# A graph layer on one core: TensorE's small products stand in four groups between its big tiles, not seven, and some work of the last pairs moves ahead

## The chip, the core and the metric

The kernel runs on one core of a Trainium2 chip. Its time is device microseconds of one execution: a median of 3041.12 us over three runs (3034.78 to 3041.24). The core's engines run side by side and wait for each other through semaphores: TensorE (PE) multiplies matrices into PSUM, VectorE (DVE) and ScalarE (ACT) work elementwise, GpSimd (POOL) issues the gathers from memory, SyncE (SP) issues most other transfers. Each engine takes its instructions in the order in which they were written, so an instruction that waits holds all behind it.

## What is computed

There are 12,500 nodes with 32 features and 400,000 edges (src, dst) sorted by dst, each with 32 features of its own.

```python
h = max(layernorm(x), 0)
e = concat(h[src], h[dst], edge_attr)            # 400000 x 96
v = relu(e @ W1 + b1) @ W2 + b2                  # 64 hidden, 32 out
out = x + max(segment_max(v, dst), h)
```

The work per edge is: fetch two rows of h, multiply 96 by 64, multiply 64 by 32, and take the maximum over the edges of one dst.

## The kernel before, in words

**Chunks.** The edges are cut into four stripes, one on each 32 partitions, and each stripe into 196 chunks of 512 edges. One pass of the main loop (`for c in range(0, NCH, 2)`, 98 passes) takes a pair of chunks c and c + 1 through the products, and prepares a = c + 2 and b = c + 3. In the text a0 to a3 and b0 to b3 are the four tiles of chunk a and of chunk b.

**Rows of src, two ways.** A chunk needs 16 x 128 rows h[src]. Twelve of the sixteen are gathered from memory by GpSimd (`gather`, L168), one indirect transfer for 128 rows, so 24 a pass. The other four are made by TensorE (`tile`, L279): the node table `hs` lies in SBUF in two parts, and a one-hot matrix `hot` picks groups of 14 nodes out of it in 14 products of 128 x 128 by 128 x 448; VectorE masks the result (L286), takes the maximum over the group (L287), and turns rows into features (`to_features`, L300 and L303). The one-hots are made by VectorE (`one_hots`, L248) and ScalarE (`one_hots_act`, L257 and L258).

**Small products.** Between these tiles TensorE does, once a pass, seven further groups:

- ea (`edges_into`, L644): W1's part for edge features of chunks a and b, into the banks `ph`; 16 records of 32 x 64 by 32 x 512.
- of (`windows_into`, L644): W1's part for h[dst], by way of one-hots `of` against the 32 rows of dst that a stripe's chunk spans.
- ht (L644): W1's part for h[src] of chunks c and c + 1; it closes the banks.
- pv (L710): W2, after ScalarE's relu (`hid`, L695).
- the transposes of `leave_1` (L551, 128 x 128): they turn the running maxima `sm` of the pair, which VectorE's scans (L717) made, from features to edges; VectorE adds b2 (L553, `so`).
- two groups of `leave_2` (L565), one for each chunk of a pair: a one-hot `last` (`lasts`, L539) picks the last edge of every dst. `leave_3` copies both results with ScalarE (L584, `wo`) and stores the spans to `top_d` with eight transfers of SP (L589). For the last eight chunks (from `LATE`) it keeps them in SBUF instead, and `late_out` scatters them into the output with GpSimd (L636).

**Order.** The order of all engines is the order of the source text: the kernel runs under a manual schedule. In the pass of before it is, on TensorE: ht, a1, pv, a2, ea, a3, L565, b0, L565, b1, of, b2, transposes, b3, a0 of the next pair. Transposes and L565 groups of a pair are thus one pass apart: the transposes of c and c + 1 stand in pass c, their L565 groups in pass c + 2. All tiles, transposes, pv results and L565 results share three PSUM buffers, `pv`.

**Waits put in by hand.** `HELD` says for some gathers of a pair after which product of an earlier pass they may start (`hold`, `passes`); the first gather waits for `of` of three passes ahead.

**End.** The nodes' rows come back from `top_d` in three shares (`rows_of`), and `finish` takes the maximum with h, adds x and stores them (L605 to L607). `finish(0)` and `finish(1)` are in pass LATE + 2, `finish(2)` in pass LATE + 4 (c = 192). After that `rows_next` gathers one span (`ew`, L623), and seven scatters of the late chunks follow (L636).

Of the kernel before, what the change touches and what calls it, by code (L numbers as in the profile page):

```python
# [24 lines left out]
P = 128  # L25
# [12 lines left out]
NCH = 196  # L38
# [16 lines left out]
LATE = NCH - 8  # L55
PIECE = 2 * A0
GP = 3
HELD = {0: (3, 'of'), 2: (3, 'b2'), 4: (3, 'b3'), 6: (3, 'n0'), 8: (2, 'ht'), 10: (2, 'a1'), 12: (2, 'pv'), 14: (2, 'a2'), 16: (2, 'a3'), 18: (2, 'lv'), 20: (2, 'b0'), 22: (2, 'b1')}
ROUND = 12582912.0
LOW = 1e30  # L60
BY_ACT = range(A1 - 3, A1)
# [10 lines left out]
def gnn_kernel(ctx, tc, x, src, src_mm, src_t, dst, dst_ext, lo, lo_c, ends_b, edge_attr, weights, w1, w2, b2, out):  # L72
# [19 lines left out]
    nc = tc.nc  # L92
# [108 lines left out]
    def passes(iteration, name, ins):  # L201

        passed[iteration, name] = ins
# [64 lines left out]
    def tile(c, m):  # L268

        if c not in MMC:  # L270
            return
        if m == 0:
            mm_rows[c] = early.tile([P, MM, D], F32, name="gm", bufs=6)
        hot = hots[c]
        e = slice(m * P, (m + 1) * P)
        po = early_ps.tile([P, C], F32, name="pv", bufs=3)[:, :D * A0]
        for k in range(A1):
            for part in range(2):
                ins = nc.tensor.matmul(po, hot[:, k, e], hs[:, part, k].rearrange("p f a -> p (f a)"),  # L279
                                 start=(k == 0 and part == 0), stop=(k == A1 - 1 and part == 1))  # L280
        if m == 0 and c % 2 == 0:
            passes(c // 2 - 2, "n0", ins)
        passes(c // 2 - 1, "ab"[c % 2] + str(m), ins)
        of_group = po.rearrange("p (f a) -> p f a", a=A0)
        one = early.tile([P, D, A0], F32, name="one", bufs=2)
        nc.vector.tensor_tensor(one, of_group, masks[c][:, m, None, :].to_broadcast([P, D, A0]), op=ALU.mult)  # L286
        nc.vector.tensor_reduce(mm_rows[c][:, m, :], one, axis=AX.X, op=ALU.max)  # L287
# [190 lines left out]
    with tc.tile_pool(name="edges", bufs=3) as pool, tc.tile_pool(name="edges_ps", bufs=1, space=PSUM) as ps:  # L478
# [57 lines left out]
        def lasts(c):  # L536
            last = pool.tile([P, J, NS, W], F32, name="last", bufs=2)
            at = ats[c // BLOCK].rearrange("p (s c) j -> p s c j", s=NS)[:, :, c % BLOCK].rearrange("p s j -> p j s")
            nc.vector.tensor_tensor(last, count_ps[:, None, None, :].to_broadcast([P, J, NS, W]),  # L539
                                    at[:, :, :, None].to_broadcast([P, J, NS, W]), op=ALU.is_equal)  # L540
            return last
# [4 lines left out]
        def leave_1(c, sm):  # L546

            px = early_ps.tile([P, C], F32, name="pv", bufs=3).rearrange("p (j q) -> p j q", j=J)
            n = blocks(c)
            for j in range(n):  # L550
                passes(c // 2, "tr", nc.tensor.transpose(px[:, j, :], sm[:, j * P:(j + 1) * P], ident))  # L551
            so = pool.tile([P, J, P], F32, name="so", bufs=2)
            nc.vector.tensor_tensor(so[:, :n], px[:, :n], b2r[:, None, :].to_broadcast([P, n, P]), op=ALU.add)  # L553
            return so

        def leave_2(c, x, sos, last):

            n = 1 + (c < NCH - 2)
            if x == 0:
                left[c] = early_ps.tile([P, C], F32, name="pv", bufs=3)[:, :n * 2 * D]  # L560
            pw = left[c]
            to = x % n * 2 * D
            for j in range(blocks(c + x)):
                for g in range(2):
                    ins = nc.tensor.matmul(pw[g * 2 * W:(g + 1) * 2 * W, to:to + 2 * D],  # L565
                                           last[x][:, j, 2 * g:2 * g + 2].rearrange("p s w -> p (s w)"),
                                           sos[x][:, j, g * 2 * D:(g + 1) * 2 * D], start=(j == 0 and x < n),
                                           stop=(j == blocks(c + x) - 1 and x >= 2 - n))
            passes(c // 2 + 1, ("lv", "lw")[x], ins)

        def leave_3(c):

            n = 1 + (c < NCH - 2)
            pw = left.pop(c)
            if c >= LATE:
                late[c] = ow = pool.tile([P, 2, D], F32, name="ow", bufs=4)
                pw = pw.rearrange("p (x k f) -> p x k f", k=2, f=D)
                for s in range(NS):
                    g = slice(s * W, (s + 1) * W)
                    nc.vector.tensor_tensor(ow[g, :n], pw[g, :, s % 2], late_x[c][g, 1, :n], op=ALU.max)  # L580
                nc.vector.tensor_tensor(ow[:, :n], ow[:, :n], late_x[c][:, 0, :n], op=ALU.add)
                return
            wo = pool.tile([P, 4 * D], F32, name="wo")
            nc.scalar.activation(wo, pw, AF.Copy)  # L584
            for x in range(2):
                base = windows.pop(c + x)
                for s in range(NS):
                    g = slice(s * W, (s + 1) * W)
                    nc.sync.dma_start(top_d[bass.ds(base[s], W), :],  # L589
                                      wo[g, (2 * x + s % 2) * D:(2 * x + s % 2 + 1) * D])  # L590
# [11 lines left out]
        def finish(i):  # L602

            r, (t, of_h) = shares.pop(i)
            nc.vector.tensor_tensor(t, t, of_h, op=ALU.max)  # L605
            nc.vector.tensor_tensor(t, t, xs[:, r], op=ALU.add)
            nc.sync.dma_start(out_v[:, r], t)  # L607
# [20 lines left out]
        def late_out(c):  # L628

            ow = late.pop(c)  # L630
            n = 1 + (c < NCH - 2)
            k = c - LATE
            if n == 1:
                nc.vector.tensor_tensor(ow[:, 0], ow[:, 0], ew, op=ALU.max)
            for x in range(n):
                nc.gpsimd.indirect_dma_start(  # L636
                    out=out[:, :], out_offset=bass.IndirectOffsetOnAxis(ap=late_o[:, k + x:k + x + 1], axis=0),
                    in_=ow[:, x, :], in_offset=None)
# [8 lines left out]
        def edges_into(c):  # L647

            if c < NCH:
                two = [ps.tile([P, 2, C], F32, name=f"ph{k}") for k in range(NS // 2)]  # L650
                ph = [two[s // 2][:, s % 2] for s in range(NS)]
                banks[c] = two
                passes(c // 2 - 1, "ea", into_ph(ph, [(w1c, loaded[c + x][0]) for x in range(2)], True, False))
                return ph

        def windows_into(c, ph):
            if c < NCH:
                passes(c // 2 - 1, "of", into_ph(ph, [(spans[c // 2][:, x], ofs.pop(c + x)) for x in range(2)],
                                                 False, False))
# [9 lines left out]
        ph = edges_into(0)  # L669
# [10 lines left out]
        for c in range(0, NCH, 2):  # L680
# [6 lines left out]
            if c % LOAD and b_next < NB and b_next not in ats and b_next not in loaded_b:  # L687
                load_block(b_next)

            ht = [hts.pop(c + x).rearrange("p k e -> p (k e)") for x in range(2)]  # L690
            passes(c // 2, "ht", into_ph(ph, [(w1a, ht[x]) for x in range(2)], False, True))
            hid = []
# [8 lines left out]
                flag = nc.values_load(general_i[0:1, 0:1], min_val=0, max_val=P)  # L701
            one_hots_act(b)
            one_hots(b, 0, 2)
            tile(a, 1)
            to_features(a, 1)
            pv = [early_ps.tile([P, C], F32, name="pv", bufs=3) for x in range(2)]
# [12 lines left out]
                sms.append(sm)  # L719
            tile(a, 2)  # L720
            to_features(a, 2)
            last = [lasts(c - 2 + x) for x in range(2)] if c else []
            ph = edges_into(a)
            one_hots(b, 2, BY_ACT.start)
            mask_of(b)
            tile(a, 3)
# [1 line left out]
            load_keys(a + KEYS)  # L728
            to_features(a, 3)
            to_features(a, J)  # L730
            if c:
                leave_2(c - 2, 0, so, last)
            if c == LATE + 4:
                finish(2)
            tile(b, 0)
            to_features(b, 0)
            if c:
                leave_2(c - 2, 1, so, last)
                leave_3(c - 2)
            one_hots(a + 2, 0, 2)  # L740
            if c == LATE + 2:
                finish(0)
            tile(b, 1)
            to_features(b, 1)
            windows_into(a, ph)
            one_hots(a + 2, 2, BY_ACT.start)
            mask_of(a + 2)
            tile(b, 2)
            to_features(b, 2)
            so = [leave_1(c + x, sms[x]) for x in range(2)]  # L750
            if c == LATE:
                half = LOAD * C // 2
                db = pool.tile([P, LOAD * C], I32, name="db", bufs=2).bitcast(F32)
# [36 lines left out]
        for ins, at in waiting:  # L790
            if at not in passed:
                continue
            tc.add_manual_dep(ins.ins, passed[at].ins.name,
                              mybir.DependencyInfo(mybir.DependencyClass.Sync, mybir.DependencyReason.DATA))
        last = [lasts(NCH - 2 + x) for x in range(2)]
        late_out(LATE + 4)
        for x in range(2):
            leave_2(NCH - 2, x, so, last)
        leave_3(NCH - 2)
# [145 lines left out]
```

## Time and profile before

| | |
|---|---|
| median of three runs | 3041.12 us |
| the profiled execution | 3041.33 us, span of its instructions 3039.6 us |
| TensorE busy (matmul) | 2941.8 us, 97% |
| GpSimd busy | 2239.7 us, 74% |
| VectorE busy | 2147.8 us, 71% |
| ScalarE busy | 1330.9 us, 44% |
| mean granted clock of TensorE | 0.986 |

Lines of the order of time give start, length, engine, line of the source, operation, the tile written and those read, and in brackets the idle time of the engine before it and what ended it. Successive instructions of one kind are merged (x14). A matrix product's length overlaps with the next one's start, so the distance between starts tells what a group costs. An fp32 product on TensorE leaves two records here, so the eight calls of a small group stand as x16. Lines of a stretch (A:B) give its length and each engine's busy time in it with the count of instructions, then TensorE's granted clock.

### The profile page before, as it was taken

How to read it: one execution, taken by the hardware profiler on the slowest of the kernel's cores; microseconds unless marked ns; L12 is line 12 of the kernel's file. 1: busy time of each engine (PE TensorE's matmuls, PEld its weight loads, DVE VectorE, ACT ScalarE, POOL GpSimd, SP SyncE). 2: the span in 40 equal slices, each digit the busy share in tenths (PEclk: the TensorE clock that was granted, in tenths of full speed). 3: DMA queues.
4: the chain of work that ended last, by engine and by line, in shares of the span. 5: the costliest groups of instructions: out<-in, count | busy, mean ns of one | idle time of the engine just before them, and what ended most of it. 6: DMA issues, size and time to landing. Idle time of an engine off the chain costs nothing. (4 is left out here: it accounts for less than half of the span.)

```text
span 3039.6 us, 59462 instructions
## 1 busy us (share of the span) xinstructions
PE 2941.8 (97%) x21067; PEld 2280.2 (75%) x21067; DVE 2147.8 (71%) x3885; ACT 1330.9 (44%) x1977; POOL 2239.7 (74%) x2380
## 2 busy tenths in 40 slices
PE   2899999999999999999999999999999999999997
PEld 1677777777777777777777777777777777777775
DVE  5577767677777676777777776777777767777666
ACT  3444444444444444444444444444444444444432
POOL 7677777777777777777777777777777777777762
PEclk7899999999999999999999999999999999999998
DMA  5422222222222223222222222222222222222222
GB/s 200 106 73 71 77 63 75 70 73 66 78 78 64 70 72 81 59 73 75 74 62 77 70 77 64 74 70 73 69 80 75 59 76 74 77 60 75 67 56 70
DMA packets 188988, 228.10 MB, mean 75 GB/s; under 512 B 119037, under 2 KB 160397, under 8 KB 175886
## 3 DMA queue, kind: packets, MB, share of 16 engines
q10 hardware_dynamic: 25076, 107.07, 11.0%
q0 software_dynamic: 75552, 38.83, 8.7%
q1 hardware_dynamic: 88058, 78.37, 8.3%
q8 instruction: 165, 2.70, 0.4%
q14 instruction: 137, 1.12, 0.1%
HBM read 211.79 MB, written 12.22 MB: 74 GB/s over the span
## 5 line engine op out<-in xcount | busy, mean ns | idle before, releaser
L168 POOL DMA_INDIRECT gh<-h_d,src_i x2321 | 2192.8, 945 | 734.0 <-issue 564.5
L279 PE MATMUL pv<-hs,hot 128*128 128x448 f32 x10808 | 2355.1, 370 | 0.9 <-DVE one L286 0.9
L279 PEld LDWEIGHTS pv<-hs,hot 128*128 128x128 f32 x10808 | 1979.0, 188 | 464.8 <-DVE one L286 234.9
L286 DVE TENSOR_TENSOR one<-pv,mask 128x448 f32<-128x448 f32 x772 | 482.2, 625 | 781.2 <-PE pv L279 772.6
L258 ACT ACTIVATE hot<-away,ones 128x512 fp32r<-128x512 f32 x579 | 418.8, 723 | 429.3 <-issue 409.5
L695 ACT ACTIVATE hid<-ph,wt 128x1024 f32<-128x1024 f32 x196 | 207.7, 1111 | 767.5 <-PE ph L644 761.6
L287 DVE TENSOR_REDUCE gm<-one 128x32 f32<-128x448 f32 x772 | 478.8, 620 | 26.5
L248 DVE TENSOR_TENSOR hot<-kb,consts 128x1024 fp32r<-128x1024 f16 (+1 forms) x385 | 458.2, 1190 | 0.0
L257 ACT ACTIVATE away<-kb,key_n 128x512 f32<-128x512 f16 x579 | 410.7, 709 | 0.0
L717 DVE TENSOR_TENSOR_SCAN sm<-pb,sm,pv 128x512 f32<-128x512 bf16 x195 | 245.0, 1257 | 18.9 <-PE pv L710 8.3
L300 DVE STREAM_TRANSPOSE ht<-gh 128x96 f32<-128x96 f32 x774 | 207.8, 268 | 0.0
L533 ACT ACTIVATE of<-db,below 128x512 f32<-128x512 int32 x196 | 139.5, 712 | 102.4 <-PE ph L644 97.7
L565 PEld LDWEIGHTS pv<-so,last 128*64 128x64 f32 x3128 | 107.5, 138 | 64.7 <-issue 64.7
L534 ACT ACTIVATE of<-of,ones 128x512 f32<-128x512 f32 x196 | 141.9, 724 | 6.4
L565 PE MATMUL pv<-so,last 128*64 128x64 f32 x3128 | 134.2, 229 | 4.5 <-DVE last L539 4.5
L644 PE MATMUL ph<-of,qw 32*64 32x512 f32 x1568 | 111.4, 617 | 24.1 <-ACT of L534 24.1
L644 PE MATMUL ph<-ea,wt 32*64 32x512 f32 x1568 | 110.1, 617 | 20.7 <-DMA qf<-q_d 20.7
L531 ACT ACTIVATE qw<-qf 128x128 f32<-128x128 f32 x98 | 30.4, 310 | 226.2 <-DMA top_d<-wo 127.3
L553 DVE TENSOR_TENSOR so<-pv,wt 128x512 f32<-128x512 f32 x196 | 122.3, 663 | 3.4 <-PE pv L551 3.3
L539 DVE TENSOR_TENSOR last<-consts,at 128x512 f32<-128x512 f32 x196 | 122.5, 663 | 0.0
L644 PE MATMUL ph<-ht,wt 32*64 32x512 f32 x1568 | 113.0, 622 | 3.2 <-DVE ht L306 3.2
L710 PE MATMUL pv<-hid,wt 64*32 64x512 f32 x1568 | 109.5, 606 | 2.7 <-ACT hid L695 2.7
(93 smaller groups left out, 599.6 us busy)
## 6 DMA issues: line engine op xcount, KB each, us to landing
ea<-in_edge_attr SPq DMA_DIRECT2D x49, 1024.0 KB
db<-in_dst_ext ACTq DMA_DIRECT2D x48, 1024.0 KB
gh<-h_d,src_i POOLq DMA_INDIRECT x2321
pb<-pen_d ACTq DMA_DIRECT2D x48, 512.0 KB
kb<-key_d ACTq DMA_DIRECT2D x47, 512.0 KB
qf<-q_d SPq DMA_DIRECT2D x784, 8.0 KB
top_d<-wo SPq DMA_DIRECT2D x752, 4.0 KB
q_d<-qs SPq DMA_DIRECT2D x6, 512.0 KB
```

The source lines that it names most:

```text
L168: ins = nc.gpsimd.indirect_dma_start(out=parts[-1][:, i, :], out_offset=None, in_=h_d[:, :], in_offset=bass.IndirectOffsetOnAxis(ap=src_i[ ...
L248: nc.vector.tensor_tensor(hot_of(c)[:, start:stop], keys[c][:, None, :].to_broadcast([P, n, MM * P]), key_ps[:, start:stop, None].to_broad ...
L257: nc.scalar.activation(away, keys[c], AF.Square, bias=key_n[:, k:k + 1])
L258: nc.scalar.activation(hot_of(c)[:, k], away, AF.Relu, bias=ones, scale=-1.0)
L279: ins = nc.tensor.matmul(po, hot[:, k, e], hs[:, part, k].rearrange("p f a -> p (f a)"), start=(k == 0 and part == 0), stop=(k == A1 - 1 a ...
L286: nc.vector.tensor_tensor(one, of_group, masks[c][:, m, None, :].to_broadcast([P, D, A0]), op=ALU.mult)
L287: nc.vector.tensor_reduce(mm_rows[c][:, m, :], one, axis=AX.X, op=ALU.max)
L300: nc.vector.transpose(ht[:, r].rearrange("p k e -> p (k e)"), gh[c][part][:, :r.stop - r.start].rearrange("p k f -> p (k f)"))
L565: ins = nc.tensor.matmul(pw[g * 2 * W:(g + 1) * 2 * W, to:to + 2 * D], last[x][:, j, 2 * g:2 * g + 2].rearrange("p s w -> p (s w)"), sos[x ...
L644: ins = nc.tensor.matmul(ph[s][x * HID:(x + 1) * HID], w[g], e[g], start=start, stop=stop)
L695: nc.scalar.activation(two, of, AF.Relu, bias=b1c)
L717: nc.vector.tensor_tensor_scan(sm[:, :n], loaded.pop(c + x)[2][:, :n], pv[x][:, :n], before, op0=ALU.add, op1=ALU.max)
```

## The change

On TensorE the pass is now: transposes of the pair before and ht; a1; pv; a2, a3; ea and the first L565 group; b0, b1; of and the second L565 group; b2, b3, a0 of the next pair. Line by line:

- `leave_1` moves from behind b2 to the beginning of the next pass, ahead of ht. The last pair has its own call behind the loop.
- `edges_into` moves from between a2 and a3 to behind a3, next to the first `leave_2`.
- the second `leave_2` and `leave_3` move from behind b0 to behind `windows_into`, ahead of b2.
- `lasts` is called for c and c + 1 there too, for use one pass later, instead of behind a2 of the pass that uses it.
- `finish(2)` moves from behind a3 to behind a2 of its pass; `finish(0)` from behind b0 to ahead of it.
- in the last pass the L565 groups, `leave_3` and `late_out` of chunks 192 and 193 stand ahead of pv, and `lasts` of the last two chunks behind them.
- in `HELD` the first gather of a pair waits for the second L565 group instead of `of`.

```diff
-HELD = {0: (3, 'of'), 2: (3, 'b2'), ...
+HELD = {0: (3, 'lw'), 2: (3, 'b2'), ...
...
+            so = [leave_1(c - 2 + x, sms[x]) for x in range(2)] if c else []
             ht = [hts.pop(c + x).rearrange("p k e -> p (k e)") for x in range(2)]
             passes(c // 2, "ht", into_ph(ph, [(w1a, ht[x]) for x in range(2)], False, True))
...
+            if c == NCH - 2:
+                for x in range(2):
+                    leave_2(c - 2, x, so, last)
+                leave_3(c - 2)
+                late_out(c - 2)
+                last = [lasts(c + x) for x in range(2)]
             tile(a, 1)
...
             tile(a, 2)
             to_features(a, 2)
-            last = [lasts(c - 2 + x) for x in range(2)] if c else []
-            ph = edges_into(a)
+            if c == LATE + 4:
+                finish(2)
             one_hots(b, 2, BY_ACT.start)
...
             to_features(a, 3)
             to_features(a, J)
-            if c:
+            ph = edges_into(a)
+            if c and c < NCH - 2:
                 leave_2(c - 2, 0, so, last)
-            if c == LATE + 4:
-                finish(2)
+            if c == LATE + 2:
+                finish(0)
             tile(b, 0)
             to_features(b, 0)
-            if c:
-                leave_2(c - 2, 1, so, last)
-                leave_3(c - 2)
             one_hots(a + 2, 0, 2)
-            if c == LATE + 2:
-                finish(0)
             tile(b, 1)
             to_features(b, 1)
             windows_into(a, ph)
+            if c and c < NCH - 2:
+                leave_2(c - 2, 1, so, last)
+                leave_3(c - 2)
+            if c < NCH - 2:
+                last = [lasts(c + x) for x in range(2)]
             one_hots(a + 2, 2, BY_ACT.start)
...
             to_features(b, 2)
-            so = [leave_1(c + x, sms[x]) for x in range(2)]
...
-        last = [lasts(NCH - 2 + x) for x in range(2)]
-        late_out(LATE + 4)
+        so = [leave_1(NCH - 2 + x, sms[x]) for x in range(2)]
         for x in range(2):
             leave_2(NCH - 2, x, so, last)
```

No product, transfer or elementwise operation is added or taken away.

More of the change, by code (lines that the diff above doesn't have):

```diff
@@ L57 @@
 GP = 3
-HELD = {0: (3, 'of'), 2: (3, 'b2'), 4: (3, 'b3'), 6: (3, 'n0'), 8: (2, 'ht'), 10: (2, 'a1'), 12: (2, 'pv'), 14: (2, 'a2'), 16: (2, 'a3'), 18: (2, 'lv'), 20: (2, 'b0'), 22: (2, 'b1')}
+HELD = {0: (3, 'lw'), 2: (3, 'b2'), 4: (3, 'b3'), 6: (3, 'n0'), 8: (2, 'ht'), 10: (2, 'a1'), 12: (2, 'pv'), 14: (2, 'a2'), 16: (2, 'a3'), 18: (2, 'lv'), 20: (2, 'b0'), 22: (2, 'b1')}
 ROUND = 12582912.0
@@ L550, in leave_1 @@
             for j in range(n):
-                passes(c // 2, "tr", nc.tensor.transpose(px[:, j, :], sm[:, j * P:(j + 1) * P], ident))
+                passes(c // 2 + 1, "tr", nc.tensor.transpose(px[:, j, :], sm[:, j * P:(j + 1) * P], ident))
             so = pool.tile([P, J, P], F32, name="so", bufs=2)
```

## The prediction

> **What bounds the kernel now.** I read the page's busy shares first, then a long stretch by engine, then the order of TensorE, ScalarE, VectorE, GpSimd and SyncE over one period from the middle, then the tail.
>
> ```profile
> span 3039.6 us, 59462 instructions
> PE 2941.8 (97%) x21067; PEld 2280.2 (75%) x21067; DVE 2147.8 (71%) x3885; ACT 1330.9 (44%) x1977; POOL 2239.7 (74%) x2380
> ...
> 165.00:2860.00 2695.00, 2695.00 (x19376) 2097.58 (x19377) 1939.89 (x3506) 1204.32 (x1791) 2034.08 (x2155) 1.00 0.28 71
> ```
>
> The last line is a stretch from 165 to 2860 us: TensorE is busy 2695.00 of 2695.00 us, at full clock. So the order and form of TensorE's work sets the time. GpSimd issued 2155 gathers there: 2695.00/2155 = 1.251 us each, so it is close behind.
>
> One period of TensorE, columns start, length, instructions:
>
> ```profile
> 1499.63 3.08 PE L279 MATMUL pv<-hs,hot 128*128 128x448 f32 x14
> 1502.54 1.04 PE L551 MATMUL pv<-ident,sm 128*128 128x128 f32 x8
> 1503.42 5.88 PE L279 MATMUL pv<-hs,hot 128*128 128x448 f32 x28
> 1509.23 1.11 PE L644 MATMUL ph<-ht,wt 32*64 32x512 f32 x16
> 1510.27 3.08 PE L279 MATMUL pv<-hs,hot 128*128 128x448 f32 x14
> 1513.28 1.09 PE L710 MATMUL pv<-hid,wt 64*32 64x512 f32 x16
> ...
> 1521.36 0.69 PE L565 MATMUL pv<-so,last 128*64 128x64 f32 x16
> 1521.98 3.08 PE L279 MATMUL pv<-hs,hot 128*128 128x448 f32 x14
> ...
> 1528.62 1.11 PE L644 MATMUL ph<-of,qw 32*64 32x512 f32 x16
> 1529.66 2.67 PE L279 MATMUL pv<-hs,hot 128*128 128x448 f32 x12
> ```
>
> Lengths overlap, so I take distances between starts. The period is 1529.66 - 1499.63 = 30.03 us. A tile (14 products) takes 1513.28 - 1510.27 = 3.01 between two groups of small shape; 1502.54 - 1499.63 = 2.91 when the full-size transposes follow; two in a row take 1509.23 - 1503.42 = 5.81. With t for a bare tile, r for starting again after a group and x for leaving into a smaller shape: t + r = 2.91, t + r + x = 3.01, 2t + r + x = 5.81. So t = 2.80, r = 0.11, x = 0.10. Those two are what an interruption costs beside its own products.
>
> **The change, part by part.** The sum is made against the profiled execution, 3041.33 us (span 3039.6 and 1.7 around it), 0.2 above the median of 3041.12.
>
> *Tiles.* Before, seven starts r (after the transposes, ht, pv, ea, two L565 groups, of) and six leavings x. After, the runs are a1 | a2 a3 | b0 b1 | b2 b3 a0: four r, three x. That is 3 x 0.11 + 3 x 0.10 = 0.63 less.
>
> *Joins.* The transposes now stand before the ht products, ea before the first L565 group, of before the second. Unlike groups stand side by side once in the trace of before, where chunk 195 has no tiles:
>
> ```profile
> 3005.92 1.15 PE L565 MATMUL pv<-so,last 128*64 128x64 f32 x32
> 3007.00 1.11 PE L644 MATMUL ph<-of,qw 32*64 32x512 f32 x16
> 3008.05 1.09 PE L551 MATMUL pv<-ident,sm 128*128 128x128 f32 x8
> 3009.07 1.07 PE L644 MATMUL ph<-ht,wt 32*64 32x512 f32 x2
> ```
>
> 32 products of L565 take 1.08 up to the next group, 16 take 0.62 up to a tile; the second 16 add 0.46, which leaves 0.16 for leaving, whether to a tile or to `of`. `of` takes 1.05 to the transposes and 1.04 to a tile. So leaving one small group for another costs what leaving it for a tile costs, and the group entered pays nothing more. Transposes to ht take 1.02 against 0.88 to a tile: 0.14 more. Bounds for the two joins: 0 by these rows, though they show L565 to `of` and not the two new directions; 2 x (0.11 + 0.10) = 0.42 if both changes of shape cost what they do at a tile. I take 0, since those rows are groups of the same shapes. Saving: 0.63 - 0.14 = 0.49 us a period. It is whole for c = 2 to 190, 95 periods: 46.5 us.
>
> The Trainium skill, TensorEngine Tiling (Array Packing), section Key Properties, says that a change of tiling mode drains TensorE, while another tile of the same mode does not. By that rule the two joins, which do change mode, keep a drain each, against 0 by the row above; it is a rival below.
>
> *Waits on TensorE.* PSUM tiles `pv` come from three buffers; order of release matters, since the second L565 group now stands directly before b2 and its result is held until ScalarE has copied it (L584). The built order shows b2 waiting for VectorE alone and a0, two tiles later, for ScalarE. That is two tiles, 5.6 us, for this:
>
> ```profile
> 1525.72 0.28 ACT L584 ACTIVATE wo<-pv 128x128 f32<-128x128 f32 x1 [0.74 <-PE pv L565]
> 1500.51 0.31 ACT L531 ACTIVATE qw<-qf 128x128 f32<-128x128 f32 x1 [4.55 <-DMA top_d<-wo]
> 1510.38 2.12 ACT L695 ACTIVATE hid<-ph,wt 128x1024 f32<-128x1024 f32 x2 [6.82 <-PE ph L644]
> ```
>
> The copy ends 1526.00, 1.01 after its group's start of 1524.99 (1521.98 + 3.01). Cost 0; without that cover 1.01 - 0.62 = 0.4 a period. a3 now follows a2 at once and needs the first scan out of its buffer: in the rows below the two scans start 1.5 after pv (1514.78 - 1513.28) and take 1.3 each, so the first ends 2.8 after pv starts; a3 starts 1.0 + 2.9 = 3.9 after it.
>
> *VectorE.* The two additions after the transposes (L553, 1.25 us) move behind a0's reduction; one-hots of last edges (L539) move behind the second L565 group. In before VectorE waits for TensorE ahead of most reductions:
>
> ```profile
> 1504.13 1.25 DVE L553 TENSOR_TENSOR so<-pv,wt 128x512 f32<-128x512 f32 x2
> 1513.39 0.62 DVE L286 TENSOR_TENSOR one<-pv,mask 128x448 f32<-128x448 f32 x1 [1.49 <-PE pv L279]
> 1514.78 2.62 DVE L717 TENSOR_TENSOR_SCAN sm<-pb,sm,pv 128x512 f32<-128x512 bf16 x2
> ```
>
> The additions take 1.25 of a gap of 1.49, which the 0.9 of the transposes on TensorE widens. The one-hots stand behind b1's reduction, 1.4 long (1513.39 to 1514.78), while TensorE does `of` and L565 (1.04 + 0.62), so their buffer is free when they come; the next two tiles, 5.6, cover them. Cost 0; if either sticks out, at most the 1.25 of such a pair, a period.
>
> *Stores of spans.* L584 moves from 16.5 us after the ht start (1525.72 - 1509.23) to 20.1 (ht 1.04, a1 3.01, pv 1.0, two tiles 5.81, ea 1.04, L565 0.62, two tiles 5.81, of 1.04, L565 0.7), and eight stores on SP with it; the loads of q and the next spans stand behind them:
>
> ```profile
> 1465.96 25.29 SPq L589 DMA_DIRECT2D top_d<-wo  x8
> 1492.01 3.96 SPq L518 DMA_DIRECT2D qf<-q_d  x8
> ```
>
> Every second period this train lasts 25 us, and `qw` waits 4.55 for the loads, which holds ScalarE. Shifted by 3.6 us, and the period 0.5 shorter, the 6.82 before `hid` becomes 2.7. Cost 0; see the slower rival.
>
> *Gathers.* The first gather of a pair now waits for the second L565 group, 0.6 us after `of`. GpSimd's own pace decides more:
>
> ```profile
> 1500.79 0.94 POOL L168 DMA_INDIRECT gh<-h_d,src_i  x1 [0.30 <-issue]
> 1508.28 0.94 POOL L168 DMA_INDIRECT gh<-h_d,src_i  x1 [0.30 <-issue]
> 2866.16 0.94 POOL L168 DMA_INDIRECT gh<-h_d,src_i  x1 [2.67 <-PE ph L644]
> 2870.97 0.94 POOL L168 DMA_INDIRECT gh<-h_d,src_i  x1 [2.62 <-PE pv L279]
> 2960.07 0.94 POOL L168 DMA_INDIRECT gh<-h_d,src_i  x1 [5.60 <-PE pv L279]
> 2975.36 0.94 POOL L168 DMA_INDIRECT gh<-h_d,src_i  x1 [0.30 <-issue]
> 3011.38 0.24 DVE L300 STREAM_TRANSPOSE ht<-gh 128x64 f32<-128x64 f32 x1
> ```
>
> The first two rows are six gathers apart: 1.248 each, 29.96 for the 24 of a period, above TensorE's new 29.54. But the last gather ends 35.1 us before use. TensorE may gain that, less a landing (estimated at no more than the 3.8 from the store at 3010.21 to the gather at 3013.96 in the tail's rows below), plus the waits that GpSimd loses (2695 - 2155 x 1.248 = 5.6 in the stretch, then 4.7 around 2870 and 5.3 at 2960): 31.3 + 15.6 = 46.9. So 46.5 just fits. Cost 0, at worst the 15.6.
>
> *Two stalls.* At 2950 L551 waits 4.15 us for L584, itself held behind a key load; afterwards two tiles take 7.4 instead of 5.9:
>
> ```profile
> 2954.31 1.19 PE L551 MATMUL pv<-ident,sm 128*128 128x128 f32 x8 [4.15 <-ACT wo L584]
> 2955.16 7.44 PE L279 MATMUL pv<-hs,hot 128*128 128x448 f32 x28
> ```
>
> Here a0 inherits the wait. L551 stood 23.3 us after the ht start (1502.54 + 30.03 - 1509.23), a0 will stand at 25.7 (20.0 and two tiles), while the loads of SP come up to 2 us later. I take no change; bounds -5.7 and +3. The wait for the check's maximum at c = 182 stays.
>
> *Tail.* `finish(2)` moves ahead of a3's reduction, and the chain out of it sets the end:
>
> ```profile
> 2993.63 1.27 PE L644 MATMUL ph<-ht,wt 32*64 32x512 f32 x16
> 3007.61 1.25 DVE L605 TENSOR_TENSOR hot<-hot 128x1088 f32<-128x1088 f32 x1
> 3010.21 0.34 SPq L607 DMA_DIRECT2D out<-hot  x1
> 3013.96 0.94 POOL L623 DMA_INDIRECT ew<-out,late_i  x1 [37.66 <-SPq L807]
> 3029.37 0.19 DVE L634 TENSOR_TENSOR ow<-ow,ew 128x32 f32<-128x32 f32 x1
> 3033.38 0.96 POOL L636 DMA_INDIRECT out<-ow,late_o  x1 [1.94 <-POOLq L807]
> ```
>
> Its store lands, `ew` is gathered, and seven scatters follow, each behind the one before: 19.4 us. In before it starts 14.0 us after ht of c = 192. In after it needs a2's reduction alone: ht 1.04, a1 3.01, pv 1.0, a2 2.91, then its masking, reduction and transpose 1.4, and 0.1 to be seen: 9.5. That is some 4.4 us sooner (bounds 0, if its loads are late, and 5). The last scatter's rows stood ready 3.8 us before it (3029.37 + 0.19 to 3033.38); the one-hots and spans of the last pairs, moved out of that path (1.25 of L539 and as much of L565), take at least 2.5 off it, so 3.8 + 2.5 - 4.4 leaves it ready in time.
>
> **Sum.** 3041.3 - 46.5 - 4.4 = 2990.4; I say 2991.
>
> **Rivals.** (a) *Joins keep a drain.* If a change of shape inside a group costs what it costs at a tile's edge, 0.42 of the 0.49 goes: 7 us and 4.4 remain, 3030; with half of it (one of the two sides), 0.28 x 95 + 4.4 = 31, 3010, which I take. The rows at 3006 speak against it, though in the other direction. The Trainium skill's rule on tiling modes, named above, is this mechanism.
> (b) *GpSimd becomes the bound.* If its 1.251 with waits is its own pace, a period cannot fall below 30.02 once the lead is used up: 31.3 + 4.4 gained, 3006. For it speaks how full GpSimd is, against it the single rows at 1.248.
> (c) *Slower: the store train on SP.* Beside the 2.7 left ahead of `hid` there is 0.9 of cover on TensorE (a tile of 3.01 over the 2.12 of `hid`). If `qw` comes more than 3.6 later than the 3.6 assumed, TensorE waits every second period, 47 times, and another 1.0 (the gain of two periods) breaks even. At 2 us beyond cover: 47 x 2 - 51 = 43 slower, 3084; the clock may fall in such gaps as it did at 2955. For it speaks that the train fills SP, against it that the change adds no bytes and no stores.
> (d) *Nothing moves*, since r and x are hidden elsewhere or a new wait takes them; the seamless 5.81 speaks against it. 3041.
>
> **Chances.** Forecast 0.62, 2983 to 3000; (a) 0.12; (b) 0.12; (c) 0.10; (d) 0.04. 0.2% (6 us) is about what a measurement tells from no change. Faster 0.62 + 0.12 + 0.12 = 0.86, same 0.04, slower 0.10. The range reaches from the forecast without the stall at 2950 (2985, less 3 for the rounding of r and x) to (a) with three quarters of the drains (3020).
>
> **What would show it.** A period of 29.5 us in TensorE's order; two tiles in a row at 5.8 for a2 a3 and b0 b1; ea to L565 at 1.04 and L565 after `of` at 0.62; no wait of a0 for L584; GpSimd's waits for TensorE gone and its lead shrunk to a few us; L605 on `hot` 9 to 10 us after the last full ht. Wrong if ea to L565 takes 1.2 or more, if `hid` or a0 waits for ScalarE, or if VectorE waits for gathers before the end.

## The result, and the profile after

The median fell from 3041.24 us (five runs, 3034.78 to 3043.55) to 3005.52 us (five runs, 3003.71 to 3008.03). The ratio is 0.9885, 95% interval 0.9871 to 0.9900: 1.15% faster. The sign was forecast, the size was not: 50 us were forecast, 36 came. On some of the chips that ran experiments the kernel before itself took 3635 to 3676 us, and the traces taken there show pauses on all engines for which the profile names no releaser. So each run below is compared only with the kernel before on its own chip.

The changed kernel's profiled execution took 3006.03 us. From its page, the span and the busy shares:

```profile
span 3004.3 us, 59483 instructions
PE 2896.6 (96%) x21067; PEld 2300.7 (77%) x21067; DVE 2149.3 (72%) x3885; ACT 1324.8 (44%) x1977; POOL 2239.2 (75%) x2380
```

TensorE is less busy than before by 45 us, which is about the saving that was forecast, but the span fell by only 35. Two stretches of the run show that the gain has a time limit:

```profile
165.00:1800.00 1635.00, 1635.00 (x11956) 1306.73 (x11955) 1198.46 (x2162) 741.07 (x1109) 1235.44 (x1309) 1.00 0.28 72
1800.00:2780.00 980.00, 970.75 (x7063) 772.71 (x7062) 706.36 (x1278) 438.88 (x655) 740.45 (x785) 1.00 0.28 72
```

From 165 to 1800 us TensorE never pauses. From then on it is idle for 9.25 us of 980, while GpSimd (last busy column) issues 785 gathers: 980/785 = 1.248 us each, its own pace, and 24 x 1.248 = 29.96 us a pass.

I took the start of the pv products of each pass in both traces and followed the difference between them. After less before, in us:

| stretch | forecast | measured |
|---|---|---|
| start to the first pv | 0 | -3.0 |
| c = 0 to 120 | 59 x -0.49 = -28.9 | -31.4 |
| c = 120 to 182 | 31 x -0.49 = -15.2 | -1.3 |
| c = 182 to 184, the check's maximum | -0.5 | +2.4 |
| c = 184 to 188 | 2 x -0.49 = -1.0 | -1.1 |
| c = 188 to 190, where L551 had waited for L584 | -0.5 | -5.2 |
| c = 190 to 192 | -0.5 | +5.9 |
| c = 192 to the end | -4.4 | -1.7 (-3.2, then +1.5) |
| sum | -51.0 (the prediction's 46.5 and 4.4; it says 50) | -35.3 |

The mean period is 29.54 us from c = 4 to 120 (before 30.05), then 30.00 up to c = 182 (before 30.04). The 3.0 at the start precede the first of the moved steps that repeat; this time differs between executions (the first pv starts at 100.0 us before, at 97.0 after, at 94.9 and 99.1 in two variants below).

One undisturbed period of TensorE:

```profile
1500.98 8.68 PE L279 MATMUL pv<-hs,hot 128*128 128x448 f32 x42
1509.50 1.04 PE L551 MATMUL pv<-ident,sm 128*128 128x128 f32 x8
1510.46 1.11 PE L644 MATMUL ph<-ht,wt 32*64 32x512 f32 x16
1511.51 3.08 PE L279 MATMUL pv<-hs,hot 128*128 128x448 f32 x14
1514.52 1.09 PE L717 MATMUL pv<-hid,wt 64*32 64x512 f32 x16
1515.54 5.88 PE L279 MATMUL pv<-hs,hot 128*128 128x448 f32 x28
1521.35 1.11 PE L644 MATMUL ph<-ea,wt 32*64 32x512 f32 x16
1522.40 0.69 PE L565 MATMUL pv<-so,last 128*64 128x64 f32 x16
1523.01 5.88 PE L279 MATMUL pv<-hs,hot 128*128 128x448 f32 x28
1528.83 1.11 PE L644 MATMUL ph<-of,qw 32*64 32x512 f32 x16
1529.87 0.69 PE L565 MATMUL pv<-so,last 128*64 128x64 f32 x16
```

The next three tiles start at 1530.49, so this period is 29.51. From the start of ea to L565 it is 1.05, from `of` to L565 1.04, from L565 to a tile 0.61 and 0.62, and nothing waits. ScalarE in the same period, then ScalarE and the pv products in the next one, in which the stores of spans hold its loads:

```profile
1501.10 0.28 ACT L584 ACTIVATE wo<-pv 128x128 f32<-128x128 f32 x1 [5.63 <-PE pv L565]
...
1511.62 2.12 ACT L696 ACTIVATE hid<-ph,wt 128x1024 f32<-128x1024 f32 x2 [7.17 <-PE ph L644]
...
1539.77 0.31 ACT L531 ACTIVATE qw<-qf 128x128 f32<-128x128 f32 x1 [4.24 <-DMA top_d<-wo]
...
1542.72 2.10 ACT L696 ACTIVATE hid<-ph,wt 128x1024 f32<-128x1024 f32 x2
1544.03 1.92 PE L717 MATMUL pv<-hid,wt 64*32 64x512 f32 x16
```

The copy L584 is done 0.4 us after the three tiles b2, b3 and a0 have begun, and none of them waits for it. `hid` has 7.17 us of idle time ahead of it in the first of these passes and none in the second: there `qw` has waited for its loads, `hid` starts 2.75 us after ht (1539.97) and not 1.16, and the pv products stand for 1.92 us and not 1.09.

Now the same order of time around 2400 us, by GpSimd, ScalarE's queue, VectorE and TensorE; the first row is the first wait of this kind:

```profile
1812.30 0.28 DVE L300 STREAM_TRANSPOSE ht<-gh 128x96 f32<-128x96 f32 x1 [0.50 <-DMA gh<-h_d,src_i]
...
2397.21 0.56 ACTq L506 DMA_DIRECT2D db<-in_dst_ext  x1
2397.81 0.52 ACTq L507 DMA_DIRECT2D pb<-pen_d  x1
...
2398.95 0.94 POOL L168 DMA_INDIRECT gh<-h_d,src_i  x1 [0.30 <-DMA gh<-h_d,src_i]
...
2406.97 0.28 DVE L300 STREAM_TRANSPOSE ht<-gh 128x96 f32<-128x96 f32 x1 [2.51 <-DMA gh<-h_d,src_i]
...
2410.14 5.88 PE L279 MATMUL pv<-hs,hot 128*128 128x448 f32 x28 [0.58 <-DVE one L286]
```

VectorE (L300) waits 2.51 us for the gather of 2398.95, which left GpSimd at 2399.89 and was there 7.1 us later. TensorE then waits for VectorE to free a buffer. From the start of the pv products at 2408.01 to this tile it is 2.13 us, where 1.02 is usual; so only about half of the loss shows as idle time. VectorE's waits of 0.5 us and more for a gather come 18 times from 1812 to 2828 us, one in every second pass, 59.7 us apart on the mean. Seventeen of them are on a gather issued between 0.4 us before and 1.4 us after ScalarE's load of `pb`, which follows that of `db` (1,536 KB together); the first is on one issued 3.1 us after. The 18 were there 6.5 to 8.6 us after GpSimd had ended them. Other gathers were used as early as 4.7 us after without a wait.

The lead can be followed in the rows, as the shortest time from the end of a gather to the start of the L300 that uses it. Over 60 us each, it is 28.2 us from 350 us on, 17.8 from 1000, 9.7 from 1500 and 4.7 from 2400. In the kernel before it is never under 33.4 us between 165 and 2780 us.

### The profile page after: what moved, and what is told of

It is laid out like the page before. It is cut to its first block, busy times and chain, and to the rows that moved or that the text cites. A ratio compares the mean times of both kernels' runs of the same rounds, so it can differ in the third digit from the quotient of the medians.

```text
span 3004.3 us, 59483 instructions
## 1 busy us (share of the span) xinstructions
PE 2896.6 (96%) x21067; PEld 2300.7 (77%) x21067; DVE 2149.3 (72%) x3885; ACT 1324.8 (44%) x1977; POOL 2239.2 (75%) x2380
## 5 line engine op out<-in xcount | busy, mean ns | idle before, releaser
L279 PE MATMUL pv<-hs,hot 128*128 128x448 f32 x10808 | 2274.3, 367 | 9.9 <-DVE one L286 8.8
L584 ACT ACTIVATE wo<-pv 128x128 f32<-128x128 f32 x94 | 26.1, 278 | 599.8 <-PE pv L565 327.3
L300 DVE STREAM_TRANSPOSE ht<-gh 128x96 f32<-128x96 f32 x774 | 207.8, 269 | 39.9 <-DMA gh<-h_d,src_i 39.9
L565 PEld LDWEIGHTS pv<-so,last 128*64 128x64 f32 x3128 | 106.9, 137 | 157.0 <-issue 79.5
L565 PE MATMUL pv<-so,last 128*64 128x64 f32 x3128 | 133.7, 228 | 0.1
L717 PE MATMUL pv<-hid,wt 64*32 64x512 f32 x1568 | 116.1, 601 | 3.3 <-DVE so L553 2.8
```

Of the source, the lines that this page charges most:

```text
L300: nc.vector.transpose(ht[:, r].rearrange("p k e -> p (k e)"), gh[c][part][:, :r.stop - r.start].rearrange("p k f -> p (k f)"))
```

## Experiments

**The joins by themselves.** Two kernels make one join each from the kernel before; a third moves the transposes alone.

```diff
@@ e2_ea_join, against before
-            ph = edges_into(a)
             one_hots(b, 2, BY_ACT.start)
...
             to_features(a, J)
+            ph = edges_into(a)
             if c:
                 leave_2(c - 2, 0, so, last)
@@ e3_of_join, against before
-            if c:
-                leave_2(c - 2, 1, so, last)
-                leave_3(c - 2)
             one_hots(a + 2, 0, 2)
...
             windows_into(a, ph)
+            if c:
+                leave_2(c - 2, 1, so, last)
+                leave_3(c - 2)
@@ e1_transposes, against before
+            so = [leave_1(c - 2 + x, sms[x]) for x in range(2)] if c else []
             ht = [hts.pop(c + x).rearrange("p k e -> p (k e)") for x in range(2)]
...
-            so = [leave_1(c + x, sms[x]) for x in range(2)]
```

> The kernel before, with one part of the change: the transposes stand at the beginning of the next pass, ahead of ht. Theory (a start r and a leaving x cost 0.11 and 0.10, and transposes ahead of ht 0.14 instead): the period in the middle falls from 30.04 by 0.11 + 0.10 - 0.14 = 0.07 to 29.97 us, 3035 us in all. Rival (the position of the transposes frees TensorE from a wait): more than 0.2 less.

> The kernel before, with one part of the change: the ea products stand behind a3, next to the first L565 group. Theory: one start and one leaving less, the join of unlike shapes free, so the period falls by 0.21 to 29.83 us; GpSimd's lead pays for it over the whole run (96 x 0.21 = 20 of some 33 us), so about 3021 us. Rival (a change of shape drains inside the group): the period stays within 0.05 of 30.04.

> The kernel before, with one part of the change: the second L565 group and its copy and stores stand behind the of products. Theory: 0.21 less a period, 29.83 us, about 3021 us, no wait of a tile for the copy L584. Rival (drain inside the group): within 0.05 of 30.04. Rival (the copy's buffer is not back in time): a wait of 0.4 a period, 30.2 us or more.

They ran on a chip with the pauses: 3648.04, 3679.34 and 3752.70 us in one run each, against 3670.70 for before. The pauses differ from run to run by more than the 7 to 30 us in question, so the times decide nothing. For the joins, the orders of TensorE between pauses do, first with the ea join, then with the `of` join; what the transposes save by themselves stays undecided:

```profile
1507.05 1.11 PE L644 MATMUL ph<-ea,wt 32*64 32x512 f32 x16
1508.09 0.69 PE L565 MATMUL pv<-so,last 128*64 128x64 f32 x16
1508.71 3.08 PE L279 MATMUL pv<-hs,hot 128*128 128x448 f32 x14
```

```profile
1508.49 1.11 PE L644 MATMUL ph<-of,qw 32*64 32x512 f32 x16
1509.53 0.69 PE L565 MATMUL pv<-so,last 128*64 128x64 f32 x16
1510.15 2.41 PE L279 MATMUL pv<-hs,hot 128*128 128x448 f32 x10
```

In both it is 1.04 from the group's start to L565 and 0.62 from L565 to the tile, the values that each group had next to tiles. A join keeps no cost beside that of leaving the group, and rival (a) falls. By the rule of the Trainium skill on tiling modes (TensorEngine Tiling (Array Packing), section Key Properties), as the prediction reads it, some further time was to show at each join; none does. A tile behind a group is a change of shape too, so this doesn't tell whether TensorE drains at both.

**Fewer gathers.** One more block of 128 rows per chunk is left out of the gathers. VectorE fills its place with rows that TensorE made for other edges, so the values of those edges are wrong and only the times count. GpSimd issues 22 gathers a pass and not 24; its own pace is then 27.5 us a pass.

```diff
@@ e5_after_22 (against after) and e4_before_22, e7_before_22 (against before)
-        n = min(K - MM * (c in MMC), (SE - c * C) // D)
+        n = min(K - (MM + 1) * (c in MMC), (SE - c * C) // D)
...
+            nc.vector.transpose(ht[:, n], gm[:, 0])
```

> The changed kernel with 22 gathers a pair of chunks instead of 24: one row in twelve is left out and its place filled from a row that TensorE made, so the values of those edges are wrong. Theory (the gathers take the last third of the gain, once GpSimd's lead is used up): the period stays at 29.51 up to pass 90, some 14 us less than the changed kernel at its 3005.5, so 2988 to 2993 us, and the gathers' lead does not shrink. Rival (TensorE slows down after pass 60 for another reason): the period rises to 30.0 there all the same, 3005 us.

2986.59 us (2981.50 to 2993.51, four runs) against 3037.32 for before on the same chip: 0.9836, interval 0.9815 to 0.9857. The trace is of the fastest of the four. Its second stretch:

```profile
1800.00:2780.00 980.00, 980.00 (x7172) 783.86 (x7171) 722.55 (x1366) 442.97 (x661) 690.18 (x731) 1.00 0.28 71
```

TensorE's idle 9.25 us are gone, and it does 7172 products in the second stretch, not 7063. The period is 29.52 up to c = 120 and 29.52 from there to c = 182, where the changed kernel has 30.00. VectorE waits for gathers nowhere, and the shortest time from a gather's end to its use stays at 34.3 us or more. Up to c = 120 this trace is 2.7 us ahead of the changed kernel's, at c = 182 17.3, at c = 184 21.6: so 14.7 us were lost to GpSimd's pace and 4.3 at the check's maximum, where the reduction ahead of it also waits for a gather (below). This is the experiment that settles where the missing gain went. It took nothing off TensorE.

> The kernel before, with 22 gathers a pair of chunks instead of 24: one row in twelve is left out, and its place is filled from a row that TensorE made, so the values of those edges are wrong. GpSimd's own pace is then 22 x 1.249 = 27.5 us a pair. Theory (before is bound by TensorE alone): the period stays 30.04 and the time within 6 us of 3041. Rival (GpSimd had a share in the period before): the period falls below 29.9.

> The kernel before with 22 gathers a pair of chunks instead of 24 (one row in twelve left out, its place filled from a row that TensorE made, so the values of those edges are wrong), on an undisturbed chip. Theory (before is bound by TensorE's order alone): period 30.04, time within 5 us of before. Rival (GpSimd already had a share in before): 29.9 or less, more than 10 us faster.

The control, the same edit to the kernel before, was meant to show that gathers cost nothing there. Both runs fell on chips with the pauses: 3457.65 against 3670.70 us, and 3452.83 (3443.00 to 3458.07) against 3666.84, ratio 0.9407, interval 0.9384 to 0.9430. Fewer gathers are worth 6% there, for a reason that has nothing to do with this change. On an undisturbed chip the control was not obtained; that before is not held by gathers rests on its trace (TensorE 2695.00 of 2695.00 us busy, no gather used less than 33.4 us after its end).

**A longer lead.** If the lead of GpSimd is a stock that is used up, more of it at the beginning must move the break to a later pass. Without the waits put in by hand GpSimd starts further ahead.

```diff
-HELD = {0: (3, 'lw'), 2: (3, 'b2'), 4: (3, 'b3'), 6: (3, 'n0'), ...
+HELD = {}
```

> The changed kernel without the waits that were put in by hand ahead of gathers (an empty table HELD): a gather then waits for its buffer alone. Theory (GpSimd is the bound, and its waits cost what they last): the waits of some 10 us over 1.25 a gather go, the lead at the start is up to 10 us longer, and the time falls by 5 to 10 us, 2995 to 3001. Rival (the hand-made waits cost nothing, or keep gathers out of the way of large loads): within 3 us of 3005, or above it.

2994.96 us (2994.61 to 2998.50, four runs), ratio 0.9856 (0.9839 to 0.9873) against before on that chip. GpSimd alone from 50 to 165 us, in the changed kernel:

```profile
50.00:165.00 115.00, 81.86 (x87) 0.82 0.41 110
```

and without the waits:

```profile
50.00:165.00 115.00, 86.95 (x92) 0.82 0.41 110
```

Five gathers more are five times 1.248 = 6.2 us more of lead by then. From 350 to 410 us the shortest time from a gather's end to its use is 37.3 us, against 28.2: 9.1 more. The first wait of VectorE for a gather then comes at 2401.81 us (c = 156), not 1812.30 (c = 116), and the period from c = 120 to 182 is 29.68 on the mean, between 29.52 and 30.00. The theory of a stock is borne out by its size: 20 passes at some 0.47 us are 9.4. The span is 7.6 us shorter than the changed kernel's (2996.7 against 3004.3), though the intervals of the two ratios, measured on two chips, just touch.

**The place of finish(0).** In the changed kernel's last passes VectorE meets a load that it didn't meet before. The rows, from the check's maximum to the end:

```profile
2828.04 0.28 DVE L300 STREAM_TRANSPOSE ht<-gh 128x96 f32<-128x96 f32 x1 [2.79 <-DMA gh<-h_d,src_i]
2829.06 0.56 PE L793 MATMUL pv<-worst,ones 128*128 128x1 f32 x2 [5.13 <-DVE worst L791]
...
2938.26 0.37 SPq L600 DMA_DIRECT2D db<-top_d  x1
...
2943.32 1.23 DVE L605 TENSOR_TENSOR db<-db 128x1024 f32<-128x1024 f32 x1 [6.81 <-DMA db<-h_d]
...
2957.64 0.66 PE L551 MATMUL pv<-ident,sm 128*128 128x128 f32 x4 [1.68 <-DVE one L286]
2958.22 2.45 PE L644 MATMUL ph<-ht,wt 32*64 32x512 f32 x16
...
2969.76 1.25 DVE L605 TENSOR_TENSOR hot<-hot 128x1088 f32<-128x1088 f32 x1
...
2976.23 0.94 POOL L623 DMA_INDIRECT ew<-out,late_i  x1 [18.37 <-SPq L813]
2998.09 0.96 POOL L636 DMA_INDIRECT out<-ow,late_o  x1 [1.93 <-POOLq L813]
```

`finish(0)` stands ahead of b0's reduction now, and SP issued its loads only at 2938.26 and after. VectorE, with b0 and all behind it, waits 6.81 us; TensorE then waits for VectorE three times, 2.45, 0.17 and 1.68 us. One edit puts it back behind b0:

```diff
-            if c == LATE + 2:
-                finish(0)
             tile(b, 0)
             to_features(b, 0)
             one_hots(a + 2, 0, 2)
+            if c == LATE + 2:
+                finish(0)
```

> The changed kernel with one line back where it was: finish(0) behind b0 in pass 190, not ahead of it. Theory (there VectorE waited 6.8 us for the node rows, which held b0's reduction and then TensorE; the pass took 37.2 us): that pass falls to 30 to 31.5 us, the last pass starts with TensorE at full clock, and the time falls by 6 to 8 us, 2997 to 3000. Rival (the wait comes back at another instruction of that pass, the reduction of b1 or finish(1)): within 3 us of 3005.

> The changed kernel with finish(0) behind b0 in pass 190, as in an earlier run, on another chip. Theory (VectorE's wait of 6.8 us for node rows made pass 190 37.2 us long): the pass falls to 30 to 31.5 us and, where TensorE does not pause without a releaser, the time to 2997 to 3000 us (ratio to before 0.986 to 0.987). Rival (the wait comes back in that pass): pass 190 above 34 us, 3003 us or more. On a chip with such pauses: a ratio of 0.993 as in the earlier run, and only the distance from ht of pass 192 to the end can be read (41.6 against the 46.1 of the changed kernel).

Both runs fell on chips with the pauses: 3642.60 us (3638.22 to 3646.98) against 3666.84, ratio 0.9934 (0.9917 to 0.9952), and on another 3651.76 (3646.49 to 3656.61) against 3676.42, ratio 0.9939 (0.9925 to 0.9952). The end of the first:

```profile
3582.37 1.21 DVE L605 TENSOR_TENSOR db<-db 128x1024 f32<-128x1024 f32 x1
...
3594.79 1.56 PE L644 MATMUL ph<-ht,wt 32*64 32x512 f32 x16
...
3604.80 1.25 DVE L605 TENSOR_TENSOR hot<-hot 128x1088 f32<-128x1088 f32 x1
...
3630.27 0.96 POOL L636 DMA_INDIRECT out<-ow,late_o  x1 [1.93 <-POOLq L813]
```

The wait ahead of `finish(0)` is gone in both, and from ht of c = 192 to the end of the span it is 41.65 and 43.12 us (46.04 in the changed kernel, 45.92 in before). But the place alone doesn't decide it: in the next experiment `finish(0)` stands there too, and VectorE waits. What the place is worth in total wasn't shown: the changed kernel itself wasn't run on such a chip, nor this one on an undisturbed chip.

**The tail's order undone.** As above, and with `finish(2)` back behind a3 and b0, the last pair's steps in their old places too.

```diff
@@ e9_tail_old, against e8_finish0_late
-            if c == NCH - 2:
-                for x in range(2):
-                    leave_2(c - 2, x, so, last)
-                leave_3(c - 2)
-                late_out(c - 2)
-                last = [lasts(c + x) for x in range(2)]
...
-            if c == LATE + 4:
-                finish(2)
             one_hots(b, 2, BY_ACT.start)
...
-            if c and c < NCH - 2:
+            if c:
                 leave_2(c - 2, 0, so, last)
+            if c == LATE + 4:
+                finish(2)
```

> The changed kernel with the order of the last passes as in the kernel before: finish(0) and finish(2) in their old places, no special order of the last pass. Theory (finish(2) earlier is worth 4.4 us at the end): 4 to 5 us slower than the run with finish(0) alone put back. Rival (the end is set by the scatters' own pace or by the last scatter's rows): within 2 us of that run.

3643.53 us (3642.61 to 3646.77), ratio 0.9935 (0.9913 to 0.9957), not to be told from the kernel above in total, where 4 to 5 us were expected. Its end:

```profile
3582.97 0.37 SPq L600 DMA_DIRECT2D db<-top_d  x1
...
3587.98 1.23 DVE L605 TENSOR_TENSOR db<-db 128x1024 f32<-128x1024 f32 x1 [3.84 <-issue]
...
3600.42 1.55 PE L644 MATMUL ph<-ht,wt 32*64 32x512 f32 x16
...
3613.43 1.25 DVE L605 TENSOR_TENSOR hot<-hot 128x1088 f32<-128x1088 f32 x1
...
3638.82 0.96 POOL L636 DMA_INDIRECT out<-ow,late_o  x1 [1.94 <-POOLq L808]
```

L605 on `hot` starts 13.0 us after ht here and 10.0 in both runs with the new order; the last scatter starts 38.4 us after here, 35.5 and 36.9 there. So the new order brings L605 forward by 3.0 us and the end by 2.9 and 1.5, in single traces. The loads of `finish(0)` were issued from 5.0 us before L605 on `db` here (5.1 in the changed kernel), 9.5 and 7.2 us before it in the two runs above; and VectorE waits 3.84 us here, up to the last completion event of the load at 3587.90.

**Both mends at once.** No waits by hand, and `finish(0)` late: from the two experiments above this should have been the best form.

> The changed kernel without the waits put in by hand ahead of gathers, and with finish(0) behind b0. Theory (the two costs are separate: the gathers' lead, and the stall in pass 190): the gains add up, 9 to 12 and 6 to 8 us less than the changed kernel, 2986 to 2990 us. Rival (a GpSimd with more lead exposes nothing else, but the stall of pass 190 hides in waits for gathers): 2993 to 2997, as without those waits alone.

> The same kernel as in the run before (no waits put in by hand ahead of gathers, finish(0) behind b0), on another chip. Theory (gathers' lead and the stall in pass 190 are separate costs, and TensorE's pauses without a releaser belong to the chip of the run before): pass 190 falls from the 35.1 us of the run without those waits alone to 30 to 31.5, finish(2) starts 10 us after ht of pass 192, the time is 2986 to 2990 us. Rival (the stall moves to another instruction of that pass): 2993 to 2997 us. Rival (the version itself brings the pauses): over 3040 us.

It fell twice on chips with the pauses, and there it is much slower than before, against what was expected but for the last rival (over 3040 us, which before exceeds there too): 4139.09 us (4133.68 to 4144.88) against 3666.84, ratio 1.1287 (1.1264 to 1.1310), and 4047.71 (4034.20 to 4054.10) against 3635.19, ratio 1.1122 (1.1062 to 1.1182). The waits of GpSimd, first with the waits by hand, then without them, on the first of these chips:

```profile
POOL gh L168 <- PE pv L279: 231.9, 181, 2.4
POOL gh L168 <- DVE ht L300: 13.4, 43, 0.6
```

```profile
POOL gh L168 <- DVE ht L300: 1161.8, 340, 7.9
```

Without the waits by hand GpSimd runs ahead until it waits for gather buffers, 1161.8 us in all. On an undisturbed chip taking them out gains about 0.3% (0.9856 against 0.9885); with them out the kernel loses 11 to 13% to before here. The two mends together on an undisturbed chip were not measured. I would not take them out.

## Why the prediction was right, and where it was wrong

**Right by the range, for another reason.** 3005.5 us lies above the forecast's 2983 to 3000 and inside the range up to 3020. That upper part was opened for joins that keep a drain, and the joins keep none; what filled it is the gathers' pace of rival (b), which stood at 3006. So it is luck that this range holds the time. Two of the prediction's own signs of being wrong came as well: VectorE waits for gathers, and a0 once waits for ScalarE.

**Right: the price of an interruption.** t, r and x gave 29.54 for the new period; 29.51 was measured, 29.54 on the mean with what disturbs it. The saving of 0.52 is 0.03 above the 0.49 of the sum, within the rounding of its rows; the transposes take 0.96 to ht where 1.02 was taken.

**Right: joins cost 0.** 1.05, 1.04, 0.61 and 0.62, here and in two kernels that make them singly. Rival (a) falls with them.

**Right in the main: no new wait of TensorE or VectorE in the period.** a3 does not wait for the scans, and the additions and one-hots stick out nowhere as long as the gathers are in time. a0 waits for L584 once in the run, 0.87 us at 2919.12. The remainder ahead of `hid` was mis-sized: in the 44 passes between 165 and 2780 us that have the store train it is 1.6 us on the median, not 2.7, and nothing in five. In three of them (361, 1011 and 1543 us) `hid` starts 1.3 to 1.6 us late, and the pv products behind it take 0.5, 0.5 and 0.8 us longer. This is the mechanism of rival (c), a late `qw`, at 1.8 us in all and not at 2 us in every second pass; it is the difference between 29.51 and 29.54.

**Wrong: "So 46.5 just fits. Cost 0, at worst the 15.6."** This is the step that failed, and it cost 19 us: 14.7 by pace, 4.3 at the check's maximum. That GpSimd's pace is 29.96 a pass and its lead 35.1 us was right. Two terms of the sum were not. First, the landing: 3.8 was taken, from one store in the quiet tail, but what counts is the slowest landing that recurs, 6.5 to 8.6 behind the loads of `db` and `pb`. The trace of before has it too, as the last section shows. That leaves 26.5 to 28.6 of the 35.1. Second, the 15.6 of waits that GpSimd was to lose: 10 of them lie behind c = 182, after the lead has run out, and can't pay for passes that are over; of the 5.6 in the stretch, 2695 - 2157 x 1.248 = 3.1 stayed. The sum should have been 27.6 + 2.5, about 30 us, reached after some 60 passes, and 31.4 were gained up to c = 120. This is rival (b): its 3006 rests on the same lead, with the mechanism as described there, "once the lead is used up"; its premise of 1.251 with waits is wrong, as the pace is the 1.248 of the single rows.

**Wrong in part: "Two stalls."** "I take no change" at 2950: the wait of L551 for L584 went, a0 inherited 0.87 of it, and 5.2 us were gained, near the lower bound of -5.7. The check's maximum was to stay; it grew by 2.4.

**Missing: finish(0).** The move from behind b0 to ahead of it was given no cost. Its loads are issued by SP at their own time, and the pass with its wait of 6.81 us on VectorE took 5.9 longer than before, to which the slow clock after TensorE's gaps adds. So the last passes won 5.2 and lost 5.9. That all of the 5.9 comes from this one line is not shown, since no run on an undisturbed chip moved it.

**Wrong in part: the tail, "some 4.4 us sooner".** The mechanism is there: 3.0 for L605 in the kernels above, of which 2.9 and 1.5 reached the last scatter. In the changed kernel L605 came 11.5 us after ht (2969.76 - 2958.22) where 9.5 was forecast. The 2.0 are in the rows: from ht to pv it takes 6.0 (2964.24 - 2958.22), against 4.1 in the middle of the run, because the granted clock was low after TensorE's gaps. The scatters, of which the change says nothing, took 21.9 us from `ew` to the last (19.4 in before, 19.0 in the kernel with `finish(0)` late); why they differ stays open. Net, 1.7 from pv of c = 192 on, and nothing from ht on (46.04 us to the end, 45.92 in before).

## What to carry to other kernels

A lead between two engines of nearly equal pace is a stock, spent once: take its length less the worst landing that recurs, divide by the difference of the paces, and see whether the passes end first. A wait that is saved late can't pay for passes that are over. Look for the slowest landing behind the large loads, not for a typical one. Count each moved consumer of a load as a step of its own: here one line moved ahead by one tile met a wait of 6.8 us. And where every second pass is different, read an idle time in both kinds of pass.

## What the runs showed of the hardware

*Landing.* Gathers of 128 rows that are issued next to two loads of 1,536 KB together landed 6.5 to 8.6 us after their engine's end, where others were there by 4.7. The trace has sixteen completion events for each gather, and they tell the landing where nothing waits. In before, for the gathers issued from 0.5 us before to 1.5 us after one of the 43 loads of `pb` between 165 and 2780 us, the twelfth event is there by 3.0 us, but the last comes 6.5 to 8.5 us after the engine's end (79 of 80; one record is incomplete). For gathers issued more than 20 us after such a load the last comes after 1.4 us on the median. So the slow landing follows every one of these loads, and 3.8 us could have been checked before; that the loads cause it is read from this, no run moved them.

The Trainium skill, DMA: Bandwidth & Descriptors, section Anatomy of one DMA, gives about 2.0 us plus bytes/436e3 for one transfer that GpSimd issues; an estimate by it is 2.0 for the gather alone and 3.6 more if all 1,536 KB go first at the same rate. The median of 1.4 us after an issue of 0.94 agrees in the main with the 2.0; the measured 7.1 after the engine's end is above the sum of 5.6.

*Clock.* After the gaps of 2.45, 0.17 and 1.68 us, the last at 2957, the granted clock falls:

```profile
2955.00:2958.00 3.00, 1.32 (x10) 1.01 (x9) 2.93 (x4) 0.94 (x2) 2.26 (x3) 1.00 0.10 21
2958.00:2965.00 7.00, 7.00 (x49) 3.82 (x47) 3.73 (x9) 2.12 (x2) 0.00 (x0) 0.76 0.71 232
```

TensorE is busy for 1.32 of 3 us, and the granted clock of the next 7 us is 0.76; from ht to pv it takes 2.0 us more than in the middle of the run. Such gaps don't always do that: with the tail's order undone TensorE has gaps of 2.05, 0.49 and 1.69 us in the same places, is busy for 1.31 us from 3597 to 3600, and the granted clock is 1.00 from there to 3606. What decides stays open.

*Chips.* On three chips before took 20% longer, 3635 to 3676 us. There fewer gathers gained 6%, and the kernel without the waits by hand, in which more of them are in flight, lost 11 to 13%, while on an undisturbed chip the same two edits to the changed kernel gained 0.5% and 0.3% (0.9836 and 0.9856 against 0.9885). What pauses the engines there stays open.
